# A causal attention kernel on one Trainium2 core: the diagonal key tiles of a unit are worked on first instead of last

## The chip, the cores and the metric

The kernel runs on 1 core of one Trainium2 chip. A core has five engines with their own in-order instruction queues: TensorE (PE in the profile, PEld for its weight loads), VectorE (DVE), ScalarE (ACT), GpSimd (POOL) and SyncE (SP, which here only starts DMA transfers). TensorE writes into PSUM, an accumulator memory of eight banks; VectorE and ScalarE read it from there. The metric is device time in microseconds of one execution. Before the change the median of 3 runs is 1887.55 us (1886.36 to 1890.11).

## The reference, cut to what matters

One sequence of 2048 tokens of width 256 goes through attention a, a gated feed-forward layer, attention b and the same feed-forward layer again, each on a layernormed input and each added to its input. Both attentions have 16 heads of 16 features and are causal; attention a has rotary angles, biases and 4 key heads shared by 4 query heads each, attention b has 16 key heads. The feed-forward weights arrive as 4-bit codes with scales. All is float32.

```
q, k, v = x @ Wq.T (+ bq), x @ Wk.T (+ bk), x @ Wv.T (+ bv)      # split into heads
scores = einsum('bthd,bshd->bhts', q, k) * scale
scores = where(causal, scores, -inf)
probs  = softmax(scores)                                         # exp(s - max) / sum
x = x + einsum('bhts,bshd->bthd', probs, v) @ Wo.T (+ bo)
gate, up = xn @ Wg.T, xn @ Wu.T                                  # dequantized weights
x = x + ((tanh(0.798 * (gate + 0.0447 * gate**3)) * gate * 0.5 + gate * 0.5) * up) @ Wd.T
```

## The kernel before, in words

The 2048 rows are cut into 4 query blocks of 512 rows (`b` = 0 to 3), and a block into 4 tiles of 128. Heads are worked in 4 groups of 4 (`g`). A **unit** is one (b, g); each attention has 16 units, in the order of b, then g. All instructions stand in each engine's queue in the order in which Python calls them; no scheduler moves them.

The softmax takes its maximum first, so each unit's scores are computed twice.

- **Maxima tiles** (`max_steps`, `scores`, L663 to L689). For a tile of 128 queries `i` and a key block `c`, two TensorE products (L670) make the scores of two heads, up to 512 keys wide, and one VectorE reduction (L682) takes the row maximum out of PSUM. For `c == b`, the diagonal block, the tile is only (i + 1) * 128 keys wide, and four small mask products (L645) add a large negative number to the forbidden keys. There are 8 * (b + 1) such steps. `gather` (L691) combines the maxima by five small VectorE instructions; `turn` (L708) transposes them by four TensorE products (L711) and a ScalarE copy (L717) into the tile `mT`.
- **Value steps** (`value_steps`, L724 to L815). For each tile of 128 keys `kt` and half `p` of the four heads, `pair` (L750) makes the transposed scores: two products bring in the negated maxima from `mT` (L758), two add the scores (L763), and one ScalarE exponential (L775) turns them into the tile `e`. On the diagonal key tiles (the four with kt >= 4b) only queries from `q0` on are computed (512, 384, 256 and 128 columns wide), and four mask products (L645) come between scores and exponential. `values` (L729) multiplies the exponentials of the key tile before by the values (L743) and accumulates in the one PSUM bank `ps_av`; it runs after the pair of the next key tile, one half of the queries per step, or all at once where the tile is at most 256 queries wide (`few`). A unit has 8 * (b + 1) value steps: two for each key tile.
- `end` (L786) multiplies the last key tile's exponentials and copies the sums out of `ps_av` on ScalarE (L790); `divide` (L793) transposes them (L797) and divides. Both are done in the next unit, in its steps 0 and 2.

`run` (L848) weaves these: while unit n's value steps run, the maxima tiles of unit n + 1 stand between the pair and the value products of the steps, evenly over all steps but the last three, and with them other side work: the output projection of a finished block (`out_steps`), the projections of the next block (`prep_steps`), and in attention a the dequantization of the feed-forward weights. In the last step the `turn` of unit n + 1 comes first, before that step's pair.

Three things tie the engines together around the change. Pairs and maxima tiles share three PSUM buffers `ps_s` of two banks each; a new tile waits until the ScalarE exponential or the VectorE reduction of the tile that had its buffer is done. Masked tiles are put off: their mask products and what reads them are kept in `owed` and issued by `settle` (L650) at the start of a later pair, value product or masked maxima tile. And the first pair of a unit cannot start before ScalarE has written `mT`.

Query and key rows come from DRAM: `load_q` (SP queue) for the unit after the next one, `load_k` (POOL queue) when a block's keys have been projected.

In the last query block (b = 3) `run` has no next block to prepare. The feed-forward layers (`Mlp`) follow each attention.

Of the kernel before, what the change touches and what calls it, by code (L numbers as in the profile page):

```python
# [31 lines left out]
NT = TB // P  # L32
# [47 lines left out]
def tile_hybrid_layers(  # L80
# [40 lines left out]
    def ps_s():  # L121
        return psum.tile([P, 2, 512], F32, tag="s", name="ps_s", bufs=3)
# [4 lines left out]
    def ps_m():  # L127
        return psum.tile([P, 512], F32, tag="m", name="ps_m")
# [278 lines left out]
    class Attention:  # L407
# [251 lines left out]
        def max_steps(self, b, g):  # L659

            held = {}

            def scores(i, c, p):  # L663
                if not held:
                    held["mx"] = self.wk.tile([P, NT, 4, NB], F32, tag="mx", name="mx")
                w = TB if c < b else (i + 1) * P
                self.settle("max")
                pt = ps_s()
                for r in range(2):
                    nc.tensor.matmul(  # L670
                        pt[:, r, :w],
                        lhsT=self.qT[b, g][64 * r : 64 * r + 64, p, i * P : (i + 1) * P],
                        rhs=self.key_rows(c, g, p, r, slice(0, w)),
                        start=True, stop=(c < b),
                    )

                def masked():
                    self.add_mask(pt, 0, w - P)
                    reduced()

                def reduced():
                    nc.vector.tensor_reduce(  # L682
                        held["mx"][:, i, 2 * p : 2 * p + 2, c], pt[:, :, :w], AX.X, ALU.max
                    )

                if c == b:
                    self.owed.append(("max", masked))
                else:
                    reduced()  # L689

            def gather():  # L691
                self.settle()
                nm = self.wk.tile([P, NT, 4], F32, tag="nm", name="nm")
                nc.vector.tensor_reduce(
                    nm, held["mx"][:, :, :, : b + 1], AX.X, ALU.max, negate=True
                )

                to = m_pad[:, :, :, :6].rearrange("q t r (p s) -> q t p r s", s=3)
                rest = nm.rearrange("q t (p r) -> q t p r", r=2)
                nc.vector.tensor_copy(to[:, :, :, :, 0], rest)  # L700
                less = self.wk.tile([P, NT, 2, 2], F32, tag="rest", name="rest")
                nc.vector.tensor_tensor(less, rest, to[:, :, :, :, 0], ALU.subtract)
                nc.vector.tensor_copy(to[:, :, :, :, 1], less)
                nc.vector.tensor_tensor(
                    to[:, :, :, :, 2], less, to[:, :, :, :, 1], ALU.subtract
                )

            def turn():  # L708
                pt = ps_m()
                for i in range(NT):  # L710
                    nc.tensor.matmul(  # L711
                        pt[:, i * P : (i + 1) * P],
                        lhsT=m_pad[:, i].rearrange("p r c -> p (r c)"), rhs=ident_b,
                        start=True, stop=True,
                    )
                self.mT[b, g] = self.wk.tile([P, TB], BF16, tag="mT", name="mT")
                nc.scalar.copy(self.mT[b, g], pt)  # L717


            tiles = [(i, c) for c in range(b + 1) for i in range(NT)]  # L720
            steps = [lambda i=i, c=c, p=p: scores(i, c, p) for i, c in tiles for p in range(2)]
            return steps + [gather], turn

        def value_steps(self, b, g):  # L724

            nk = NT * (b + 1)
            held = {"pending": []}

            def values(half):  # L729

                self.settle()
                kt, q0, es_ = held["pending"][0]
                few = TB - q0 <= TB // 2
                if half == 1:
                    held["pending"].pop(0)
                    if few:
                        return
                elif kt == 0:
                    held["av"] = ps_av()
                own = slice(q0, TB) if few else slice(*((q0, TB // 2), (TB // 2, TB))[half])  # L740
                for j in range(4):
                    h = g if self.first else 4 * g + j
                    nc.tensor.matmul(  # L743
                        held["av"][32 * j : 32 * j + 32, own],
                        lhsT=self.vv[kt // NT][:, kt % NT, h * VW : h * VW + 32],
                        rhs=es_[j // 2][:, j % 2, own],
                        start=(kt == 0 and half == 0), stop=(kt == nk - 1),
                    )

            def pair(kt, p):  # L750
                q0 = max(0, kt - NT * b) * P
                diagonal = kt >= NT * b
                keys = slice((kt % NT) * P, (kt % NT + 1) * P)
                self.settle()
                pt = ps_s()

                for r in range(2):
                    nc.tensor.matmul(  # L758
                        pt[:, r, q0:], lhsT=sel[64 * r : 64 * r + 64, p, :],
                        rhs=self.mT[b, g][64 * r : 64 * r + 64, q0:], start=True, stop=False,  # L760
                    )
                for r in range(2):
                    nc.tensor.matmul(  # L763
                        pt[:, r, q0:], lhsT=self.key_rows(kt // NT, g, p, r, keys),
                        rhs=self.qT[b, g][64 * r : 64 * r + 64, p, q0:],
                        start=False, stop=not diagonal,
                    )
                e = self.wk.tile([P, 2, TB], F32, tag="e", name="e", bufs=4)

                def masked():  # L770
                    self.add_mask(pt, 1, q0)
                    exponentials()

                def exponentials():
                    nc.scalar.activation(e[:, :, q0:], pt[:, :, q0:], AF.Exp, scale=QK_SCALE)  # L775

                if diagonal:
                    self.owed.append(("exp", masked))
                else:
                    exponentials()  # L780
                if p == 0:
                    held["es"] = [e]
                else:
                    held["pending"].append((kt, q0, held["es"] + [e]))

            def end():  # L786
                values(0)
                values(1)
                o = pre.tile([P, TB], F32, tag="o", name="o")
                nc.scalar.copy(o, held["av"])  # L790
                held["o"] = o

            def divide():  # L793
                o = held["o"]
                pt = ps_m()
                for i in range(NT):
                    nc.tensor.transpose(  # L797
                        pt[:, i * P : (i + 1) * P], o[:, i * P : (i + 1) * P], ident
                    )
                heads = pt.rearrange("p (t j c) -> p t j c", t=NT, c=32)  # L800
                rec = small.tile([P, NT, 4], F32, tag="rec", name="rec")
                nc.vector.reciprocal(rec, heads[:, :, :, HD])
                if g == 0:
                    self.att[b] = pre.tile([P, NT, NG, 4, HD], F32, tag="att", name="att")
                nc.vector.tensor_tensor(
                    self.att[b][:, :, g], heads[:, :, :, :HD],
                    rec.unsqueeze(3).broadcast_to([P, NT, 4, HD]), ALU.mult,
                )

            steps = []  # L810
            for kt in range(nk):
                for p in range(2):
                    scored = lambda kt=kt, p=p: pair(kt, p)
                    steps.append((scored, lambda p=p: values(p)) if kt else scored)
            return steps, end, divide  # L815

        def out_steps(self, b):
# [30 lines left out]
        def run(self, extra, beside):  # L848
# [5 lines left out]
            for n, (b, g) in enumerate(units):  # L854
# [3 lines left out]
                if g == 0 and b + 1 < NB:  # L858
                    ahead = self.prep_steps(b + 1)

                    few = -(-(len(ahead) - (7 if self.first else 5)) // 2)
# [7 lines left out]
                maxima, turn = [], None  # L869
                if n + 1 < len(units):  # L870
                    maxima, turn = self.max_steps(*units[n + 1])
                else:
                    more += beside
                steps, end, divide = self.value_steps(b, g)
# [3 lines left out]
                    steps[at] = (scored, step, *summed)  # L878
                if turn:
                    scored, summed = steps[-1]  # L880
                    steps[-1] = (turn, scored, summed)
                first = len(maxima) * 3 // len(steps)
                weave(steps[:3], maxima[:first])
                weave(steps[3:], blend(maxima[first:], more) if maxima else more, rest=3)
# [96 lines left out]
    with tc.tile_pool(name="wk1", bufs=2) as wk, tc.tile_pool(name="kv1", bufs=1) as kv:  # L981
        at.wk = at.qpool = wk
        with tc.tile_pool(name="init", bufs=1) as pool:
# [13 lines left out]
            steps, turn = at.max_steps(0, 0)  # L997
# [6 lines left out]
    with tc.tile_pool(name="kv20", bufs=1, reuse_waits="tile") as kv0, tc.tile_pool(  # L1004
# [8 lines left out]
        steps, turn = at.max_steps(0, 0)  # L1013
# [60 lines left out]
```

## Time and profile before

| | |
|---|---|
| median of 3 runs | 1887.55 us |
| the profiled execution's own time | 1890.76 us |
| its span, first to last instruction | 1888.9 us |
| mean granted TensorE clock | 0.982 |
| PE busy | 1766.7 us, 94% of the span |
| DVE busy | 1123.3 us, 59% |
| ACT busy | 805.2 us, 43% |
| attention a, from its first turn of maxima to the end of its last unit's steps | about 51 to 641 us |
| attention b, likewise | about 997 to 1548 us |

The profile is one execution; its lines name the source line, the engine, the operation, the tiles (written<-read), their shapes and how often, then busy time. "Idle before" is the time in which the engine had nothing running just before such an instruction, and the arrow names what ended it. A TensorE instruction's duration covers its whole way through the pipeline, so neighbours overlap: what an instruction costs in the queue is the distance from its start to the next one's start. Times within the execution are counted from the start of its span.

### The profile page before, as it was taken

What the parts mean: (1) busy time and instruction counts of PE and PEld (TensorE: products, weight loads), DVE (VectorE), ACT (ScalarE), POOL (GpSimd) and SP (SyncE); (2) the same over time, 40 slices, a digit from 0 to 9 for tenths busy, and PEclk for the clock granted to TensorE, in tenths of its full rate; (3) what the DMA queues carried; (4) which work ended last, traced back from release to release, by engine and by line L of the source; (5) the groups of instructions that cost most, each with busy time, mean ns of one, the idle gap of its engine ahead of it and who ended that gap; (6) DMA issues with size and microseconds to landing.
All of it is one profiled execution on the core that took longest, in us unless ns stands there. A gap on an engine that the chain in (4) does not pass through costs nothing. (4 is left out here: it accounts for less than half of the span.)

```text
span 1888.9 us, 31839 instructions
## 1 busy us (share of the span) xinstructions
PE 1766.7 (94%) x13452; PEld 928.5 (49%) x13452; DVE 1123.3 (59%) x1676; ACT 805.2 (43%) x1069; POOL 239.0 (13%) x437
## 2 busy tenths in 40 slices
PE   5788889999999999999998898999999999999999
PEld 3344444444444456656564444444444444756656
DVE  4567687778786253544445667766877715363442
ACT  1334455555667531222213355556566662131221
POOL 4111321210001011112101010010000001011110
PEclk8889999999999999999998999999999999999999
DMA  4421310310101100001303232041000010000000
GB/s 100 108 60 37 68 52 23 63 35 24 35 24 35 45 6 1 1 0 42 81 1 74 62 72 54 12 90 33 15 13 2 2 46 1 11 1 11 7 6 12
DMA packets 42271, 64.24 MB, mean 34 GB/s; under 512 B 13840, under 2 KB 20880, under 8 KB 41872
## 3 DMA queue, kind: packets, MB, share of 16 engines
q1 hardware_dynamic: 33488, 45.93, 8.2%
q0 software_dynamic: 7680, 15.74, 5.0%
q8 instruction: 106, 1.74, 0.4%
q10 hardware_dynamic: 960, 0.52, 0.1%
q14 instruction: 37, 0.30, 0.1%
HBM read 44.24 MB, written 17.83 MB: 33 GB/s over the span
## 5 line engine op out<-in xcount | busy, mean ns | idle before, releaser
L682 DVE TENSOR_REDUCE mx<-ps_s 128x2 f32<-128x1024 f32 (+3 forms) x640 | 658.2, 1060 | 221.0 <-PE ps_s L645 116.0
L775 ACT ACTIVATE e<-ps_s 128x1024 f32<-128x1024 f32 (+3 forms) x640 | 571.3, 897 | 422.6 <-PE ps_s L763 244.8
L743 PE MATMUL ps_av<-e,v 128*32 128x256 f32 (+1 forms) x4608 | 365.2, 384 | 3.4 <-ACT e L775 3.4
L763 PE MATMUL ps_s<-qT,kT 64*128 64x512 f32 (+3 forms) x1280 | 341.7, 527 | 0.0
L670 PE MATMUL ps_s<-kT,qT 64*128 64x512 f32 (+3 forms) x1280 | 269.2, 423 | 52.3 <-DVE mx L682 22.8
L758 PE MATMUL ps_s<-mT,sel 64*128 64x512 bf16 (+3 forms) x1280 | 232.7, 358 | 27.3 <-ACT mT L717 10.1
L934 PE MATMUL ps_s<-xnT,wg 128*128 128x512 f32 x512 | 242.1, 595 | 0.0
L934 PE MATMUL ps_s<-xnT,wu 128*128 128x512 f32 x512 | 240.6, 592 | 0.0
L670 PEld LDWEIGHTS ps_s<-kT,qT 64*128 64x128 f32 x1280 | 130.1, 188 | 161.6 <-ACT e L775 66.5
L758 PEld LDWEIGHTS <-sel 64*128 64x128 bf16 x1280 | 75.0, 93 | 251.2 <-issue 242.3
L942 DVE TENSOR_TENSOR t<-ps_s,t 128x512 f32<-128x512 f32 x128 | 88.1, 688 | 164.5 <-POOL t L941 162.7
L940 ACT ACTIVATE t<-ps_s 128x512 f32<-128x512 f32 x128 | 76.2, 595 | 251.8 <-PE ps_s L934 251.3
L943 ACT ACTIVATE t<-t 128x512 f32<-128x512 f32 x128 | 80.6, 629 | 200.7 <-DVE t L942 200.7
L934 PEld LDWEIGHTS ps_s<-xnT,wu 128*128 128x128 f32 x512 | 97.3, 190 | 122.7 <-issue 122.7
L941 POOL TENSOR_SCALAR t<-t 128x512 f32<-128x512 f32 x128 | 79.1, 618 | 573.0 <-ACT t L940 572.5
L743 PEld LDWEIGHTS ps_av<-e,v 128*32 128x32 f32 x4608 | 95.0, 108 | 109.1 <-issue 89.5
L934 PEld LDWEIGHTS ps_s<-xnT,wg 128*128 128x128 f32 x512 | 96.0, 192 | 106.0 <-issue 104.0
L944 DVE SCALAR_TENSOR_TENSOR t<-t,ps_s 128x512 f32<-128x512 f32 x128 | 88.0, 688 | 89.0 <-ACT t L943 89.0
L763 PEld LDWEIGHTS ps_s<-qT,kT 64*128 64x128 f32 x1280 | 130.5, 199 | 0.0
L959 PE MATMUL ps_m<-wd,inter 128*128 128x256 f32 x512 | 114.5, 380 | 0.0
L959 PE MATMUL ps_av<-wd,inter 128*128 128x256 f32 x512 | 114.5, 380 | 0.0
L959 PEld LDWEIGHTS ps_av<-wd,inter 128*128 128x128 f32 x512 | 96.7, 190 | 17.1 <-issue 4.5
(125 smaller groups left out, 1179.9 us busy)
## 6 DMA issues: line engine op xcount, KB each, us to landing
qT<-h SPq DMA_DIRECT2D x256, 64.0 KB, 2.2
kT<-h POOLq DMA_DIRECT2D x96, 128.0 KB, 5.9
h<-high SPq DMA_DIRECT2D x24, 256.0 KB, 2.6
h<-low SPq DMA_DIRECT2D x24, 256.0 KB, 2.5
wd<-wd_kept SPq DMA_DIRECT2D x2, 2048.0 KB, 7.8
wd_kept<-dq_d SPq DMA_DIRECT2D x4, 512.0 KB, 2.7
out<-x SPq DMA_DIRECT2D x16, 128.0 KB, 1.7
x<-x SPq DMA_DIRECT2D x3, 512.0 KB, 5.4
```

Of the source, the lines that this page charges most:

```text
L670: nc.tensor.matmul(pt[:, r, :w], lhsT=self.qT[b, g][64 * r : 64 * r + 64, p, i * P : (i + 1) * P], rhs=self.key_rows(c, g, p, r, slice(0, w)),
L682: nc.vector.tensor_reduce(held["mx"][:, i, 2 * p : 2 * p + 2, c], pt[:, :, :w], AX.X, ALU.max)
L743: nc.tensor.matmul(held["av"][32 * j : 32 * j + 32, own], lhsT=self.vv[kt // NT][:, kt % NT, h * VW : h * VW + 32], rhs=es_[j // 2][:, j % ...
L758: nc.tensor.matmul(pt[:, r, q0:], lhsT=sel[64 * r : 64 * r + 64, p, :], rhs=self.mT[b, g][64 * r : 64 * r + 64, q0:], start=True, stop=False,)
L763: nc.tensor.matmul(pt[:, r, q0:], lhsT=self.key_rows(kt // NT, g, p, r, keys), rhs=self.qT[b, g][64 * r : 64 * r + 64, p, q0:], start=Fals ...
L775: nc.scalar.activation(e[:, :, q0:], pt[:, :, q0:], AF.Exp, scale=QK_SCALE)
L934: nc.tensor.matmul(pt[:, k, :], lhsT=w[:, c, fc * P : (fc + 1) * P], rhs=self.xnT[b][:, c, :], start=(c == 0), stop=(c == 1),)
L941: nc.gpsimd.tensor_scalar(t, t, GELU_A, 1.0, ALU.mult, ALU.add)
L942: nc.vector.tensor_tensor(t, gate, t, ALU.mult)
L943: nc.scalar.activation(t, t, AF.Tanh, scale=GELU_C)
L944: nc.vector.scalar_tensor_tensor(t, t, 1.0, gate, ALU.add, ALU.mult)
L959: nc.tensor.matmul(po[:, :D], lhsT=inter[:, fc, i * P : (i + 1) * P], rhs=wd[:, fc, :], start=(fc == 0), stop=(fc == NFC - 1),)
```

## The change

Three orders are changed; no instruction is added, removed or resized.

1. The value steps of a unit go over the diagonal key tiles first (widest, 512 queries, to narrowest, 128), then over the full key tiles. In block 0, which has only diagonal tiles, this order stays. The flags that open and close the accumulation in `ps_av` follow the new first and last tile.
2. The maxima tiles also begin with the diagonal block, now from the widest (i = 3) to the narrowest (i = 0), then the full ones.
3. In the last step of a unit the `turn` for the next unit comes after that step's pair and before its value products, not before the pair.

```
-            tiles = [(i, c) for c in range(b + 1) for i in range(NT)]
+            tiles = [(i, b) for i in reversed(range(NT))]
+            tiles += [(i, c) for c in range(b) for i in range(NT)]
...
-            nk = NT * (b + 1)
+
+            order = [*range(NT * b, NT * (b + 1)), *range(NT * b)]
...
-                elif kt == 0:
+                elif kt == order[0]:
...
-                        start=(kt == 0 and half == 0), stop=(kt == nk - 1),
+                        start=(kt == order[0] and half == 0), stop=(kt == order[-1] and (few or half == 1)),
...
-            for kt in range(nk):
+            for kt in order:
...
-                    steps.append((scored, lambda p=p: values(p)) if kt else scored)
+                    steps.append(scored if kt == order[0] else (scored, lambda p=p: values(p)))
...
-                    steps[-1] = (turn, scored, summed)
+                    steps[-1] = (scored, turn, summed)
```

## The prediction

> **What bounds the kernel now.** First the busy times of stretches, to find the stage and its engine; only the attentions are touched. The columns are engine busy times, then the granted TensorE clock. Rows: two units of block 3 with maxima (attention b), the last unit without, and a unit (1, 3), which works on the 25 maxima steps of unit (2, 0) in 16 value steps.
>
> ```profile
> 1409.10:1455.50 46.40, 45.10 (x509) 20.38 (x506) 36.70 (x39) 30.96 (x34) 0.00 (x0) 1.00 0.05 13
> 1455.50:1502.00 46.50, 45.26 (x508) 20.16 (x504) 36.72 (x39) 30.96 (x34) 0.00 (x0) 1.00 0.01 2
> 1502.00:1548.00 46.00, 45.19 (x453) 19.03 (x450) 4.92 (x16) 33.61 (x41) 1.64 (x2) 1.00 0.13 47
> 1163.50:1193.20 29.70, 25.07 (x301) 12.61 (x298) 26.03 (x31) 14.79 (x18) 0.00 (x0) 1.00 0.07 19
> ```
>
> In block 3 PE is never idle for long; in unit (1, 3) DVE is busy for 26 of 29.7 us and bounds it. Second, who PE waits for, all over the kernel (total, times, longest):
>
> ```profile
> PE ps_s L670 <- DVE mx L682: 22.8, 47, 1.2
> PE ps_s L670 <- ACT e L775: 16.1, 31, 1.2
> ...
> PE ps_s L758 <- ACT mT L717: 10.1, 29, 0.7
> ...
> PE ps_m L711 <- DVE m_pad L704: 8.3, 7, 3.5
> ```
>
> These are small: there is little to win. Third, what a tile costs on its reader, by form:
>
> ```profile
> L682 DVE TENSOR_REDUCE mx<-ps_s 128x2 f32<-128x1024 f32 x448 | 531.3, 1220 | 122.7 <-PE ps_s L670 96.8 <-PE ps_s L645 18.9
> L775 ACT ACTIVATE e<-ps_s 128x1024 f32<-128x1024 f32 x448 | 457.1, 1026 | 311.8 <-PE ps_s L763 244.8 <-PE ps_s L645 63.4 <-PE ps_s L670 0.8
> ```
>
> Fourth, the border between two units of block 3 in order of time (start, duration, engine):
>
> ```profile
> 1409.06 0.40 PE L711 MATMUL ps_m<-ident_b,m_pad 128*128 128x128 bf16 x4
> 1409.38 0.23 PE L758 MATMUL ps_s<-mT,sel 64*128 64x128 bf16 x2
> ...
> 1409.49 0.58 ACT L717 CAST mT<-ps_m 128x512 bf16<-128x512 f32 x1 [0.45 <-PE ps_m L711]
> ...
> 1409.97 0.39 ACT L775 ACTIVATE e<-ps_s 128x256 f32<-128x256 f32 x1
> 1410.13 0.39 PE L758 MATMUL ps_s<-mT,sel 64*128 64x512 bf16 x2 [0.32 <-ACT mT L717]
> ...
> 1413.33 0.51 PE L670 MATMUL ps_s<-kT,qT 64*128 64x512 f32 x2 [0.35 <-ACT e L775]
> ...
> 1414.35 0.64 PE L743 MATMUL ps_av<-e,v 128*32 128x256 f32 x8
> ```
>
> The copy into mT runs at once, because the last pair (128 queries) and its 0.39 us exponential stand behind it; PE waits 0.32 us. From turn to the value products of step 2 it is 5.29 us here, and 5.29 to 5.30 at nearly every border behind a PE-bound unit. Fifth, two value steps with no maxima tile between, in the last unit:
>
> ```profile
> 1516.27 0.39 PE L758 MATMUL ps_s<-mT,sel 64*128 64x512 bf16 x2
> 1516.82 0.64 PE L743 MATMUL ps_av<-e,v 128*32 128x256 f32 x8
> 1516.99 1.02 ACT L775 ACTIVATE e<-ps_s 128x1024 f32<-128x1024 f32 x1 [0.20 <-PE ps_s L763]
> 1517.39 0.39 PE L758 MATMUL ps_s<-mT,sel 64*128 64x512 bf16 x2
> ```
>
> Start to start, a full pair takes PE 0.55 us before value products (0.44 before a maxima tile) and a half of value products 0.57; its exponential starts 0.72 after the pair. Such steps alternate 1.12 and 1.24 us: every second one waits 0.12 us for an exponential.
>
> **The change, part by part.** Each instruction stays, so the engines' work is the same and only waits change. I lay out the new border with the distances above.
>
> *Turn behind a full pair (A).* In blocks 1 to 3 the last pair of a unit is now full. From its start: turn at 0.55, turn lasts 0.33 (1409.06 to 1409.38), value products 0.57, so PE is ready for the next unit's first pair at 1.45. ACT has that pair's exponential first in its queue, from 0.72 to 1.74, and the mT copy behind it: starts 0.10 before its end (as 1409.97 against 1409.49 + 0.58), takes 0.58, and PE follows 0.06 later, at 2.28. PE waits 0.83 instead of 0.32: +0.51. Behind it on PE stands everything of the new unit, so nothing covers it. The last three steps, now full and without maxima, bring one 0.12 wait. +0.63 for each border behind a unit of blocks 1 to 3 with a turn, 11 an attention. The four behind the DVE-bound units (1, 3) and (2, 3) are worse: there the next reduction starts 3.29 us after the last one ends. After: the last maxima tile is issued about two reductions before its own end (-2.4), then on PE 0.33 + 0.57 + 1.12 + 1.24 + 0.55 to the turn, 1.73 to the next pair, 0.44 + 0.66 to its first reduction: 4.2; +1.0 each. 18 x 0.63 + 4 x 1.0 = **+15.3**. Bounds: 0.3 a border (+7) if exponentials run ahead, 0.9 (+20) if ACT is late. I take the middle; the rows fix it closely.
>
> *Gather waits.* Five DVE instructions before the turn now have three full steps as cover. Of the L711 waits only one stands behind a PE-bound unit of blocks 1 to 3, 0.46 us; the rest is DVE-bound (counted above), in block 0 or at the very start, where it stays: **-0.5**.
>
> *Steps 0 to 2 (B).* The pair is now masked, and the maxima tile with it is 512 wide and masked. The exponential of step 1's pair starts only when step 2 begins, and step 2's maxima tile takes its buffer: 0.80 us of waiting. Before, the ACT queue (mT, two exponentials, o, two exponentials) left 1.0 us of waiting in the same stretch: 5.29, less its work (turn 0.33, short pair with masks 0.33, three pairs 1.32, three maxima tiles 1.0, few value products 0.36, transposes 0.59: 3.93), less the wait for mT. Net **0**; bounds -0.8 and +0.4 for each of 22.
>
> *Diagonal with diagonal (C).* Before, wide maxima tiles stood beside narrow pairs; now wide with wide and narrow with narrow. Going on through steps 3 to 10 in the same way, the waits are 0.02, 0.06, 0.02, 0.16, 0.11, then 0.43 and 0.64 in steps 8 and 10: behind the 128-query tile value products are few (0.36 us, or none), while full maxima tiles come at 30 side steps in 26 steps, 1.22 us of DVE each. Sum 1.4, against 0.9 in the old diagonal stretch: +0.5. The whole unit (3, 1): pair to step 11 16.9, seventeen steps as before 24.9 and one bare 1.12, two bare 2.36, last border 2.28: 47.5 against 46.4. For 6 units of block 3 +0.5; for 12 with projections beside (PE work that fills such waits) half; for 4 DVE-bound +0.3: **+7.2**. Bounds 0 and +22.
>
> *Block 0 (8 units).* There the pair was last and narrow already: with the turn behind it the next pair still comes 1.07 us after the turn. But the maxima tiles are turned round, and steps 0 to 2 get wide beside wide: step 1's and 2's tiles wait 0.4 and 0.8 us for exponentials, while at the end narrow maxima make room earlier. I take +0.5 each, **+4**; bounds -4 and +10.
>
> *Ends and beginnings.* The two last units end on a full tile, whose value products wait for its exponential: 0.72 + 1.02 + 0.06 against 1.12 of PE work, +0.65 each, **+1.3**. The very first maxima start with the wide tile: the first reduction waits longer and DVE then runs through: **+0.4**.
>
> *DMA and other queues.* None is moved on SP or POOL. The diagonal tile needs the block's keys at the start of unit (b, 3) instead of its end: kT of block 1 landed at about 1046 us for a unit that starts at 1052, the tightest: hidden, 0; without that cover one landing of 5.9 us.
>
> Sum: 15.3 - 0.5 + 7.2 + 4 + 1.3 + 0.4 = **+27.7**. The profiled execution took 1890.76, 3.2 over the median of 1887.55; the sum made on it gives 1918.5, and on the median 1915.
>
> **The clock.** Sparse PE stretches cost clock here:
>
> ```profile
> 1070.50:1074.00 3.50, 1.85 (x26) 1.12 (x18) 1.39 (x6) 1.16 (x4) 0.00 (x0) 1.00 0.05 16
> 1074.00:1077.40 3.40, 3.40 (x22) 1.51 (x20) 2.45 (x2) 2.73 (x4) 0.00 (x0) 0.50 0.40 113
> ```
>
> With PE busy 1.85 of 3.50 us the clock is halved for the next 3.4 us: at most 1.7 us of loss. The new borders hold about 0.8 of waiting in any 3.5 us, clearly denser; I add 0 to the sum and up to 1.7 at ten sparse borders to the range. The Trainium skill ("TensorE: Matmul & The Clock Gate", section "Why this matters for your kernels") has the rule that only PE-idle gaps of more than some 3 us bring the half clock. The longest wait in that stretch is 1.33 us, so this trace disagrees. By the rule the clock term is 0 in every case; by the row it can reach 17.
>
> **Rivals.**
> 1. *Only the border pays.* The waits of C vanish because projections and ring buffers smooth them, and block 0 gains its 4: +15.3 - 0.5 + 1.7 - 4 = +12.5, **1900**. For it: PE waits of this kind are short now. Against: steps 8 and 10 have no PE work to fill.
> 2. *Heavier.* DVE comes to bound block 3's full stretch, since no narrow reductions relieve it there (C at +22), and sparse borders lose clock: 28 + 15 + 8 = +51, some +50, **1938**. For it: 1.15 x 1.22 = 1.40 us of DVE a step against about 1.4 of PE. Against: full tiles met full tiles at the same rate before.
> 3. *Faster.* The start of a unit gets the 1.14 us of value products of the full last tile as cover while ACT catches up. If step 2's tile then finds its buffer free (no 0.80) and the diagonal runs without waits (no 0.9 of before), each of 22 units gains 0.63 - 1.0 - 0.9 = -1.3: -28, **1860**. It decides where the waits from last pair to step 10 fall below the 2.3 us they are now; my layout has 3.2.
> 4. *Not what it says.* The instruction order of the built program shows the new order on PE and ACT, the mT copy behind a full exponential: excluded.
>
> **How the numbers follow.** Forecast (+14 to +44) 0.66, rival 1 and down to +4 0.13, rival 2 0.09, about nothing 0.03, faster 0.09. A difference of 0.2% (3.8 us) is about what a measurement can tell from none. Faster 0.09, same 0.04, slower 0.87. The range leaves out the upper half of rival 2, the lower half of rival 1 and the faster case: 1895 to 1938.
>
> **What would show it.** In the new profile: PE L758 waiting on mT, 10 us now, at about 0.8 a border, some 20; L775 of 128x1024 directly ahead of L717 on ACT; L670 waiting on ACT e up, its longest about 0.8 in step 2; unit (3, 1) from turn to turn 47.5 us; busy time of every engine as now. I am wrong if the unit is under 46.4 us, which would mean that steps 0 to 10 wait less than I laid out, or if the granted clock falls under 0.97.

## The result, and the profile after

| | before | after |
|---|---|---|
| median of 5 runs | 1887.97 us (1886.36 to 1890.11) | 1937.57 us (1933.25 to 1939.7) |
| the profiled execution's own time | 1890.76 us | 1933.25 us |
| its span | 1888.9 us | 1931.5 us |
| granted clock of that execution | 0.982 | 0.981 |

The change makes the kernel slower by 49.6 us: a ratio of 1.026, 95% interval 1.0249 to 1.0272. The forecast was 1915, so its direction holds and its size does not: the time lies just inside the upper end of the range, at the figure of rival 2. Profile against profile the loss is 42.5 us. The profiled execution of after is the quickest of its five, and has the highest clock of them (0.981; the others 0.977 to 0.973). Of the 7.1 us between the two figures, 4.3 come from this (its time lies that far under the median of after), and 2.8 from the profiled execution of before, which lies that far over its median.

First the work. Line 1 of the page of after, with busy time, share of the span and number of instructions of each engine:

```profile
PE 1774.8 (92%) x13452; PEld 923.6 (48%) x13452; DVE 1118.3 (58%) x1676; ACT 810.5 (42%) x1069; POOL 238.5 (12%) x437
```

Within 9 us this is what each engine did before: the time is lost in waiting. The stretches that the prediction listed, from turn to turn in after (two units of block 3 with maxima, the last unit, unit (1, 3); busy times of PE, PEld, DVE, ACT and POOL, then the clock):

```profile
1448.70:1496.30 47.60, 45.34 (x506) 19.95 (x504) 36.51 (x39) 31.25 (x34) 0.00 (x0) 1.00 0.05 13
1496.30:1543.80 47.50, 45.11 (x507) 20.06 (x505) 36.52 (x39) 31.26 (x34) 0.00 (x0) 1.00 0.01 2
1543.80:1589.80 46.00, 44.89 (x457) 18.70 (x456) 4.23 (x15) 34.36 (x41) 1.65 (x2) 1.00 0.13 47
1189.60:1222.20 32.60, 27.36 (x298) 13.28 (x296) 26.12 (x31) 14.88 (x18) 0.00 (x0) 0.95 0.06 18
```

The block 3 units went from 46.4 and 46.5 to 47.6 and 47.5 us, as laid out, with the same DVE time. Unit (1, 3) went from 29.7 to 32.6 us, also with the same DVE time (26.0 and 26.1): the engine that bounds it now stands still for 6.5 us instead of 3.7. Whom PE waits for in after (total, times, longest; L670, L711 and L717 keep their numbers, the pair's L758 is now L760, L763 is L765, L743 is L745, L775 is L777, L790 is L792, L797 is L799):

```profile
PE ps_s L670 <- DVE mx L682: 36.3, 79, 1.2
PE ps_s L670 <- ACT e L777: 28.5, 45, 1.0
PE ps_s L760 <- ACT mT L717: 21.9, 32, 0.8
...
PE ps_s L760 <- ACT e L777: 10.4, 27, 0.8
...
PE ps_m L711 <- DVE m_pad L704: 2.0, 1, 2.0
```

The wait for `mT` went from 10.1 to 21.9 us (some 20 was the sign to look for), as predicted. The gather wait fell from 8.3 to 2.0, further than the 0.5 us in the sum. The waits of maxima tiles grew by 13.5 us (for reductions) and 12.4 us (for exponentials), which is more than the prediction had room for.

The border ahead of a block 3 unit in after, in order of time (start, duration, engine; idle before and its releaser in brackets):

```profile
1448.17 0.39 PE L760 MATMUL ps_s<-mT,sel 64*128 64x512 bf16 x2
...
1448.72 0.40 PE L711 MATMUL ps_m<-ident_b,m_pad 128*128 128x128 bf16 x4
...
1448.89 1.02 ACT L777 ACTIVATE e<-ps_s 128x1024 f32<-128x1024 f32 x1 [0.22 <-PE ps_s L765]
...
1449.05 0.64 PE L745 MATMUL ps_av<-e,v 128*32 128x256 f32 x8
...
1449.82 0.58 ACT L717 CAST mT<-ps_m 128x512 bf16<-128x512 f32 x1
1450.45 0.39 PE L760 MATMUL ps_s<-mT,sel 64*128 64x512 bf16 x2 [0.75 <-ACT mT L717]
...
1454.96 0.45 PE L670 MATMUL ps_s<-kT,qT 64*128 64x384 f32 x2 [0.78 <-ACT e L777]
```

The last full pair starts at 1448.17, its exponential 0.72 later, the copy into `mT` 1.65 later, the next unit's pair 2.28 later. In between PE has only the value products of 1449.05 to issue and waits 0.75. The last row is the maxima tile of step 2, with the predicted wait (0.80 laid out, 0.78 here).

Where the time went, as differences of turn-to-turn times (profile after minus profile before), beside what the prediction's terms give for the same units:

| units | predicted | measured |
|---|---|---|
| 6 of block 3 with maxima | 6 x (0.63 + 0.5) = 6.8 | 6.7 |
| 4 bound by VectorE: (1, 3), (2, 3) in both attentions | 4 x (1.0 + 0.3) = 5.2 | 12.5 |
| 12 of blocks 1 and 2 with projections beside them | 12 x (0.63 + 0.25) = 10.6 | 15.3 |
| 8 of block 0 | 4 | 9.4 |
| the rest (feed-forward, ends) | 1.2 | -1.3 |
| span | 27.8 | 42.6 |

In the terms a border belongs to the unit ahead of it; in time most of it lies behind the turn, in the next unit. Moved there, the forecast is 4 x (0.63 + 0.3) = 3.7 for the four VectorE-bound units, 10.0 for the twelve and 7.5 for the six of block 3: the gaps at the first two only widen.

### The profile page after: what moved, and what is told of

It reads as the page before. It is cut to its first block, busy times and chain, and to the rows that moved or that the text cites. A ratio compares the mean times of both kernels' runs of the same rounds, so it can differ in the third digit from the quotient of the medians.

```text
span 1931.5 us, 31836 instructions
## 1 busy us (share of the span) xinstructions
PE 1774.8 (92%) x13452; PEld 923.6 (48%) x13452; DVE 1118.3 (58%) x1676; ACT 810.5 (42%) x1069; POOL 238.5 (12%) x437
## 5 line engine op out<-in xcount | busy, mean ns | idle before, releaser
L777 ACT ACTIVATE e<-ps_s 128x1024 f32<-128x1024 f32 (+3 forms) x640 | 572.4, 896 | 473.0 <-PE ps_s L645 254.7
L745 PE MATMUL ps_av<-e,v 128*32 128x256 f32 (+1 forms) x4608 | 363.6, 384 | 4.3 <-ACT e L777 4.3
L670 PE MATMUL ps_s<-kT,qT 64*128 64x512 f32 (+3 forms) x1280 | 280.2, 432 | 77.4 <-DVE mx L682 36.3
L765 PE MATMUL ps_s<-qT,kT 64*128 64x512 f32 (+3 forms) x1280 | 340.7, 526 | 0.0
L760 PE MATMUL ps_s<-mT,sel 64*128 64x512 bf16 (+3 forms) x1280 | 232.0, 357 | 44.2 <-ACT mT L717 21.9
L670 PEld LDWEIGHTS ps_s<-kT,qT 64*128 64x128 f32 x1280 | 128.8, 188 | 190.3 <-DVE mx L682 78.4
L760 PEld LDWEIGHTS <-sel 64*128 64x128 bf16 x1280 | 73.7, 93 | 268.8 <-issue 266.3
L745 PEld LDWEIGHTS ps_av<-e,v 128*32 128x32 f32 x4608 | 99.4, 109 | 126.2 <-issue 99.1
L765 PEld LDWEIGHTS ps_s<-qT,kT 64*128 64x128 f32 x1280 | 130.2, 198 | 0.0
```

What stands on the lines that cost most here:

```text
L670: nc.tensor.matmul(pt[:, r, :w], lhsT=self.qT[b, g][64 * r : 64 * r + 64, p, i * P : (i + 1) * P], rhs=self.key_rows(c, g, p, r, slice(0, w)),
L745: nc.tensor.matmul(held["av"][32 * j : 32 * j + 32, own], lhsT=self.vv[kt // NT][:, kt % NT, h * VW : h * VW + 32], rhs=es_[j // 2][:, j % ...
L760: nc.tensor.matmul(pt[:, r, q0:], lhsT=sel[64 * r : 64 * r + 64, p, :], rhs=self.mT[b, g][64 * r : 64 * r + 64, q0:], start=True, stop=False,)
L765: nc.tensor.matmul(pt[:, r, q0:], lhsT=self.key_rows(kt // NT, g, p, r, keys), rhs=self.qT[b, g][64 * r : 64 * r + 64, p, q0:], start=Fals ...
```

## The experiments

The change has three parts: the value order (V), the maxima order (M) and the turn behind the pair (T). The first theory was that most of the loss is the border of A, a full exponential ahead of the `mT` copy. Its rivals were that the value order or the maxima order costs inside the units, wherever the turn stands.

### One part undone

**Turn first** (V and M stay):

```
-                    steps[-1] = (scored, turn, summed)
+                    steps[-1] = (turn, scored, summed)
```

> The change with its third edit undone: the turn comes before the last pair again; both orders stay new. Theory A (the border: the copy into mT stands behind a full exponential): the waits of L758/L760 on mT, 21.9 us in all, fall under 4 us, since pair (0.55) and value products (0.57) cover the 0.58 us copy, and the time falls by 22 borders x 0.83 = 18 us, to about 1919 (1913 to 1924). Theory B (the maxima order, diagonal beside diagonal, costs the time, and ScalarE and VectorE make PE wait a little later anyway): over 1930.

Measured 1914.49 us (1910.05 to 1916.6) against 1887.62 before on the same chip: ratio 1.0134 (1.0112 to 1.0157). The waits for `mT` fall from 21.9 us to 3.0 (7 times), and PE-bound units of block 3 fall back to within 0.4 us of before. In the new order the turn's place is worth 23 us. But 27 us of loss stay, with no border to blame.

**Old maxima order** (V and T stay):

```
-            tiles = [(i, b) for i in reversed(range(NT))]
-            tiles += [(i, c) for c in range(b) for i in range(NT)]
+            tiles = [(i, c) for c in range(b + 1) for i in range(NT)]
```

> The change with its second edit undone: maxima tiles in the old order (full ones first, diagonal last, narrow to wide); value order and turn are new. Theory A: the border waits stay (mT about 22 us); only the eight units of block 0 (+9.4 us in the profiles) and the 1.1 us inside each of four VectorE-bound units come back: 1920 to 1928. Theory B: most of the loss goes, 1895 to 1905.

Measured 1932.07 us (1927.38 to 1937.73), ratio 1.0235 (1.0206 to 1.0264). Only 5.5 us come back; the `mT` waits stay at 21.9 us. With V in, full maxima tiles stand beside narrow pairs, and block 3 units get longer still: attention b's (3, 0) to (3, 2) are 1.68, 1.55 and 1.47 us over before from turn to turn, against 1.09, 1.18 and 0.93 in after. Undoing M here removes one cost and adds another.

**Old value order** (M and T stay):

```
-            order = [*range(NT * b, NT * (b + 1)), *range(NT * b)]
+            nk = NT * (b + 1)
...
-            for kt in order:
+            for kt in range(nk):
```

> The change with its first edit undone: value steps in the old order (diagonal last); maxima order and turn are new. Theory A: the last pair is narrow again and its masked exponential is issued after the copy into mT, so the border is as before; what stays is block 0 and full maxima beside narrow pairs at a unit's end: 1890 to 1902. Theory B: the loss stays, 1920 to 1938.

Measured 1917.21 us (1915.12 to 1918.18), ratio 1.0153 (1.0138 to 1.0168). A clear miss: with narrow last pairs, nothing like 30 us should have been left. The theory that the border carries the loss falls in this simple form. The parts cost something each by itself.

### One part alone

So each part was put alone into the kernel before: the value order with its accumulation flags; the maxima order; and the turn behind the pair.

> Only the first edit: value steps with the diagonal first; maxima and turn as before. Theory A (the edits' costs add up; the turn behind a full pair was 20 to 23 us of it): the time of the run with old maxima order, 1932, less 22 borders x 0.9 = 1912 (1906 to 1917). Theory C (new value order costs nothing once the turn is first, the rest is the maxima order): 1887 to 1895.

> Only the second edit: maxima tiles with the diagonal first, widest first; value steps and turn as before. Theory A: the run with old value order (1917) less what the late turn costs with a narrow last pair, 22 x 0.33 = 7: about 1910; the full maxima tiles then end beside the narrow pairs of a unit's end, where VectorE (1.22 us each) has no PE work beside it. Theory C: as e1, 1914, since the value order would cost nothing. A maxima order that costs nothing would give 1888.

> Only the third edit: the turn after the last pair; both orders as before. Theory A: the last pair (0.33 us with its masks) no longer runs beside the copy into mT, so the next unit's first pair comes 0.33 us later wherever the maxima were gathered in time: 20 x 0.33 = +6.6, 1894 (1890 to 1897). If the turn's place alone were the cost: over 1905.

| edits | median, us | over before | ratio (95%) |
|---|---|---|---|
| V | 1911.37 (1910.37 to 1912.26) | +23.5 | 1.0127 (1.0113 to 1.0141) |
| M | 1909.36 (1906.25 to 1912.76) | +21.5 | 1.0111 (1.0096 to 1.0126) |
| T | 1896.74 (1892.34 to 1898.13) | +8.9 | 1.0046 (1.0031 to 1.006) |
| V, M | 1914.49 | +26.9 | 1.0134 |
| V, T | 1932.07 | +44.5 | 1.0235 |
| M, T | 1917.21 | +29.6 | 1.0153 |
| V, M, T | 1937.57 | +49.6 | 1.026 |

All three alone came out where they were expected. Two readings follow from the table by subtraction. T costs 8 to 9 us where the last pair is narrow (T alone 8.9; after M 8.1) and 21 to 23 us where it is full (after V 21.0; after V and M 22.7, or 23.1 without the difference of the two medians of before): that fits the mechanism of A, a full exponential ahead of the copy. And M costs 21.5 us on the old value order but 3.4 on the new one: V and M do not add up. The six units of block 3 with maxima show it at full clock: V alone makes them 4.1 us longer in all, M alone 2.0, both together 1.0. That diagonal beside diagonal fits better than either order against its opposite is the likely reason; no run shows it by itself.

### The copy on another engine

If ScalarE's queue is what makes the border, the copy into `mT` on VectorE should end it, with all three edits in:

```
-                nc.scalar.copy(self.mT[b, g], pt)
+                nc.vector.tensor_copy(self.mT[b, g], pt)
```

> The whole change, but the copy into mT is made by VectorE instead of ScalarE. Theory A (ScalarE's in-order queue makes the wait): VectorE is idle for some 3 us before the turn in most units, so the copy runs right behind the turn and the mT waits (21.9 us) fall under 4 us; 1937.6 - 18 = about 1919 (1913 to 1925). Theory B: over 1930.

Measured 1929.95 us (1929.45 to 1933.82), ratio 1.0227 (1.021 to 1.0244): 7.6 us better than after, less than half of what was expected (its median clock, 0.972, is the lowest of all the kernels here). The same border in this kernel:

```profile
1445.52 0.40 PE L711 MATMUL ps_m<-ident_b,m_pad 128*128 128x128 bf16 x4
...
1445.69 1.02 ACT L776 ACTIVATE e<-ps_s 128x1024 f32<-128x1024 f32 x1 [0.21 <-PE ps_s L764]
1445.85 0.64 PE L744 MATMUL ps_av<-e,v 128*32 128x256 f32 x8
1445.95 0.69 DVE L717 CAST mT<-ps_m 128x512 bf16<-128x512 f32 x1 [2.48 <-PE ps_m L711]
1446.70 0.39 PE L759 MATMUL ps_s<-mT,sel 64*128 64x512 bf16 x2 [0.21 <-DVE mT L717]
```

The copy now starts as soon as the turn is done, beside the exponential: from turn to next pair 1.18 us instead of 1.72 in after. So at this border ScalarE's queue made 0.54 of the 0.75 us. The other 0.21 stays: the turn behind the pair leaves only the value products (0.57 us in the queue) to cover the transposes' way out and a copy that takes 0.69 us on VectorE, 0.58 on ScalarE. The expectation had counted the wait as gone; all waits for `mT` fell from 21.9 to 11.1 us, half.

### Where the orders cost

Next, all three edits everywhere but in the units of the last head group (g = 3) of blocks 0 to 2, which keep the old orders and the old turn; four of these six are the VectorE-bound units of the prediction. A unit's `new` also sets the order of the maxima that are worked on beside it:

```
+                new = g < 3 or b == 3
...
+            if not new:
+                tiles = [(i, c) for c in range(b + 1) for i in range(NT)]
...
+            order = [*range(NT * b, NT * (b + 1)), *range(NT * b)] if new else [*range(NT * (b + 1))]
...
+                    steps[-1] = (scored, turn, summed) if new else (turn, scored, summed)
```

> The whole change, except in the units with g = 3 of blocks 0 to 2 (they work on the maxima of the next block, 8 tiles more than they have value steps, and VectorE bounds them); these six units keep all three old orders. Theory A (what was under-sized lies in these units: +3.53, +3.07, +2.95, +2.97 in the two later blocks and +1.52, +2.30 in block 0, by the profiles): 1937.6 - 16.3 = about 1921 (1916 to 1926). Theory E (the excess over the forecast is clock and noise, spread over all units): over 1928.

Then block 0 and the very first maxima keep the old ones as well:

```
-                new = g < 3 or b == 3
+                new = b > 0 and (g < 3 or b == 3)
```

> As the run before, and the other units of block 0 and the very first maxima keep the old orders too; new orders remain in blocks 1 to 3 with g < 3 and in the last unit. Theory A: another 5.5 us less (the six units' growth in the profiles): about 1915 (1910 to 1920); what remains is 12 units with projections beside (+15.3 in the profiles), 6 of block 3 (+6.7) and ends. Theory E: over 1924.

And last, the same with the turn first everywhere, so that the new orders stand alone in the PE-bound units of blocks 1 to 3:

```
-                    steps[-1] = (scored, turn, summed) if new else (turn, scored, summed)
+                    steps[-1] = (turn, scored, summed)
```

> As the run before (new orders only in blocks 1 to 3 with g < 3 and in the last unit), and there too the turn is first in the last step. Theory A: 18 borders lose the 0.83 us wait behind a full exponential, 15 us: 1911.6 - 15 = about 1897 (1893 to 1901); what is left over the kernel before, some 9 us, is the two orders themselves, beside projections above all. If the turn were cheap in these units (the wait made good a step later): over 1905.

Measured 1917.14 us (1913.64 to 1919.08), ratio 1.0156 (1.014 to 1.0171); 1911.64 (1909.17 to 1913.75), ratio 1.0128 (1.0115 to 1.0142); and 1891.92 (1890.15 to 1896.77) against 1889.09 before, ratio 1.003 (1.0017 to 1.0043). The first two lie in their ranges; the last lies below its range. Some 9 us were expected to be left for the two orders: where VectorE does not bound the unit, in blocks 1 to 3, they cost about 3. The border in that last kernel shows what the turn's place does there, with a full last pair in both:

```profile
1416.24 0.40 PE L711 MATMUL ps_m<-ident_b,m_pad 128*128 128x128 bf16 x4
1416.57 0.39 PE L762 MATMUL ps_s<-mT,sel 64*128 64x512 bf16 x2
...
1416.68 0.58 ACT L717 CAST mT<-ps_m 128x512 bf16<-128x512 f32 x1
1417.12 0.64 PE L747 MATMUL ps_av<-e,v 128*32 128x256 f32 x8
...
1417.69 0.39 PE L762 MATMUL ps_s<-mT,sel 64*128 64x512 bf16 x2
```

The copy runs while PE does the pair and the value products, and the next unit's pair comes 1.45 us after the turn, without a wait: exactly the 1.45 at which the prediction had PE ready. After needs 2.28 us for the same work, 0.83 more; over 18 borders 15 us, which is the difference of the two profiles (spans 1910.0 and 1894.9). By medians it is 19.7, but the median clocks differ too (0.9815 and 0.985).

An account of the 49.6 us, by differences of medians:

- the two orders in the eight units of block 0 (where only the maxima order changes) and the four VectorE-bound ones: 1914.49 - 1891.92 = 22.6; the median clocks differ here as well (0.9765 and 0.985)
- the turn behind the pair at the 18 other borders behind units of blocks 1 to 3: 1911.64 - 1891.92 = 19.7
- the turn behind the pair at the borders behind those twelve units: (1937.57 - 1911.64) - 22.6 = 3.3
- the two orders in the other units of blocks 1 to 3: 1891.92 - 1889.09 = 2.8

These four are bound to add up to 1937.57 - 1889.09, so their sum of 48.4 is no proof; the rest of the 49.6 is the difference between two medians of before. The runs behind each median spread by 4 to 7 us.

What happens in a VectorE-bound unit shows on VectorE's own rows. First unit (1, 3) of attention b in before, from the gather ahead of it to its first reductions:

```profile
1162.28 0.23 DVE L704 TENSOR_TENSOR m_pad<-rest,m_pad 128x16 bf16<-128x16 f32 x1
1165.51 4.62 DVE L682 TENSOR_REDUCE mx<-ps_s 128x2 f32<-128x1024 f32 x4 [2.99 <-PE ps_s L670]
1170.04 0.25 DVE L802 RECIPROCAL rec<-ps_m 128x16 f32<-128x16 f32 x1
```

The same in after:

```profile
1185.79 0.23 DVE L704 TENSOR_TENSOR m_pad<-rest,m_pad 128x16 bf16<-128x16 f32 x1
1192.82 3.22 DVE L682 TENSOR_REDUCE mx<-ps_s 128x2 f32<-128x1024 f32 x3 [6.79 <-PE ps_s L645]
1197.22 0.26 DVE L804 RECIPROCAL rec<-ps_m 128x16 f32<-128x16 f32 x1 [1.18 <-PE ps_m L799]
```

The turns ahead are at 1163.47 and 1189.58, so the first reduction comes 3.24 instead of 2.04 us behind the turn: the `mT` wait, and masks ahead of it, since the first maxima tile is a diagonal one. After the first three reductions VectorE runs dry once more for 1.18 us, where before it ran through: the masked maxima tile of step 2 waits 0.41 us for a put-off exponential, and its masks stand behind the transposes of `divide`. From the first reduction's start to the last one's end it is 27.46 instead of 26.39 us, and from there to the next turn 1.94 instead of 1.3. That makes 1.2 + 1.07 + 0.65 = 2.9 us, all of what this unit lost. The other three VectorE-bound units lose in the same three places: all four 1.20 to 1.25 us at the start, 0.30 to 1.78 inside and 0.50 to 1.46 at the end, 12.5 us in all.

A lower clock is not needed for it. Unit (2, 3) of attention b from turn to turn, before and after (columns as above), has the full clock and the same VectorE time in both, and still loses 3.0 us:

```profile
1317.72:1357.51 39.79, 36.34 (x412) 17.06 (x409) 35.48 (x39) 22.97 (x26) 0.00 (x0) 1.00 0.05 14
1353.33:1396.09 42.76, 38.35 (x410) 17.33 (x409) 35.47 (x39) 23.07 (x26) 0.00 (x0) 1.00 0.05 13
```

### The turn earlier instead

T puts the turn later. The opposite, in the kernel before alone, is the turn one step earlier, behind the pair of the last step but one:

```
-                    scored, summed = steps[-1]
-                    steps[-1] = (turn, scored, summed)
+                    scored, summed = steps[-2]
+                    steps[-2] = (scored, turn, summed)
```

> The kernel before with the turn one step earlier: after the pair of the last step but one and before its value products; both orders as before. Theory A (PE waits 0.32 us a border for the copy into mT because only 0.33 us of PE work stands behind the turn): value products (0.57) and the last pair (0.33) now cover the copy, the waits of L758 on mT fall from 10 us to under 4, and about 18 borders x 0.32 = 6 us go: 1882 (1879 to 1886). Theory D (the gather is not ready a step earlier): L711 waits for m_pad rise by as much, 1886 to 1892.

Measured 1886.97 us (1882.52 to 1893.89, 11 runs), ratio 0.9996 (0.9985 to 1.0007): no difference. The `mT` waits nearly vanish (1.3 us), PE-bound units are 0.4 us shorter each, but the turn now meets maxima that aren't gathered yet, above all where VectorE is late. The wait for the gather in this kernel (8.3 us, 7 times, in before):

```profile
PE ps_m L711 <- DVE m_pad L704: 17.4, 14, 3.5
```

So the step earlier was kept only where the gather is ready, in blocks 1 to 3 without g = 3:

```
+                    if b > 0 and g < 3:
+                        scored, summed = steps[-2]
+                        steps[-2] = (scored, turn, summed)
+                    else:
+                        scored, summed = steps[-1]
+                        steps[-1] = (turn, scored, summed)
```

> The kernel before with the turn one step earlier only in units of blocks 1 to 3 with g < 3, where the gather is ready by then; elsewhere as before. Theory A: the units that lost 0.4 us each in the run with the turn earlier everywhere do so again (about 14 of them) and the ones that gained waits for the gather do not: 1887.8 - 5.8 = 1882 (1879 to 1885). If run-to-run clock is all there is to see: 1887 to 1889.

Measured 1882.26 us (1879.22 to 1887.23, 12 runs) against 1887.51: ratio 0.9973 (0.9964 to 0.9981), as expected and quicker than both kernels. Waits in this kernel:

```profile
PE ps_m L711 <- DVE m_pad L704: 11.3, 11, 3.5
...
PE ps_s L758 <- ACT mT L717: 4.7, 13, 0.7
```

The `mT` waits are halved, the gather waits cost 3 us more, and 13 of the units are 0.37 to 0.47 us shorter (from one division to the next).

## Why the prediction was right or wrong

**The border (A): right in mechanism, and in size at the border that was laid out.** The layout had PE wait for `mT` 0.83 us and the next pair 2.28 us behind the last; the profile has 0.75 and 2.28. The two kernels that differ only in the turn's place there (1911.64 and 1891.92) confirm it as a cause. At the four borders behind VectorE-bound units it was not right in size (below). What the layout left out is that the value order with the turn first would have been better than before at this place: the new border against the old is +0.63, but against a turn ahead of the full pair it is +0.83. That is why T costs more behind V than the 15 us of A.

**Gather waits: too small a term, at no cost. Steps 0 to 2 (B): right.** 2.0 us of gather waits are left, those at the very start. The waits in block 0 (3.2 us before) are gone too, which the sum did not count; block 0 grew all the same. The wait in step 2 is 0.78 against 0.80.

**Diagonal with diagonal (C) in block 3: right as a net, and partly by luck.** Six units took 6.7 us more against 6.8, unit (3, 1) from turn to turn 47.6 against 47.5. But with the turn first, V and M leave these six only 1.0 us over before, 0.16 each, with a border that by the line above is 0.20 better than the old one (0.83 - 0.63). So C costs some 0.36 us a unit and not 0.5. The turn behind the pair adds 0.95, which makes the new border some 0.75 over the old one and not 0.63. Two small errors cancel.

**The VectorE-bound units: the step that failed.** The terms were +1.0 at the border behind such a unit and +0.3 inside, 5.2 us for four. They measured 12.5. The prediction had said itself that DVE bounds unit (1, 3), and then priced everything ahead of and inside it by PE's waits, scaled down. There a wait of PE counts through when the next reduction can start: in unit (1, 3) of attention b +1.2 at the unit's own beginning (priced as +0.63), +1.07 inside, where 0.3 was taken, +0.65 at its end ahead of the turn. The +1.0 at the border behind such a unit can be held against the trace: from the last reduction to the next unit's first it was to go from 3.29 to 4.2 us and went to 4.57, 5.26, 4.76 and 5.54, a mean of +1.7. In medians, the two orders in these units and in block 0 cost 22.6 us; an estimate by the clock's price below puts some 7 of these down to the lower clock of the first of the two kernels.

**Block 0: right in sign, mis-sized.** +0.5 a unit was taken, between -0.5 and +1.25; 9.4 us for eight is +1.17 each, near the upper bound. It was taken near the middle, although no row showed maxima turned round. M alone makes these eight 8.2 us longer in its profile, so the turned maxima carry most of it.

**Projection units: mis-sized.** 15.3 against 10.6. In the last kernel of "Where the orders cost" (turn first, VectorE-bound units and block 0 old) the twelve are 3.5 us over before, 0.3 each; with the border that is 0.20 better there, this puts C at some 0.5 and not at the 0.25 taken. So the half taken off for projections that fill the waits does not seem to be there, though single units lie between -3.5 and +3.2 us, and no run shows it by itself. With the turn still first and both orders new everywhere the twelve are 8.1 us over before, and the turn behind the pair brings them to 15.3. The step from 3.5 to 8.1 comes with the new orders of the units around them, and no term was laid out for it. The clock differs between these profiles (0.982, 0.976, 0.981), and how much of the steps is clock stays open.

**Ends: small.** From the last turn to the end it is 0.7 us more, against 0.65; the first turn is 0.1 later, against 0.4. From the last turn of attention a to the first of attention b it is 2.2 us less, which no term had and no run explains.

**DMA: right.** The earlier use of the new block's keys brought no wait; the one for queries is 10.4 us in after and 10.3 before.

**The clock: left at 0 in the sum, kept in the range.** Over the five runs of after the time rises by 0.8 us for each 0.001 of granted clock lost (1933.25 at 0.981, 1939.7 at 0.973). Their median clock is 0.975, against 0.983 for the kernel before; 0.008 makes some 6 us. It is an estimate, since a lower clock and a longer wait can also have one cause. The borders did stay at full clock, as argued; the windows that lost it were elsewhere (below).

**Rival 2 had the time, not the reason.** Its 1938 is the result within 1 us. But its main part, VectorE bounding the full stretch of block 3, did not happen: those units lost what the forecast said. Heavier it was, in the units that VectorE bounded already. Rival 1 is excluded by the time and by block 0, which lost 9.4 us where it was to win 4. Rival 3 is excluded by the 0.78 us in step 2. The profile's clock, 0.981, did not fall under the 0.97 named as a sign of error either; the medians show the smaller fall that the profile, as the quickest run, does not.

What stays open: why M costs 21.5 us beside the old values. Its loss is spread over block 0, the g = 3 units and the units with projections, mostly 0.2 to 2.4 us a unit, and no run separates masks that come earlier from reductions that come wide first. And the share of clock and waiting in the medians was not told apart by a run. For the VectorE-bound units the traces bound it: in after only the two units (1, 3) have half clock, 3.4 us each, at most 1.7 us of loss apiece, and M alone makes the four units 7.0 us longer without any.

## What to carry to other kernels

Price a change of order in each stage on the engine that bounds it: where VectorE is the bound, lay out when its next reduction can start, and read its own idle time, not PE's waits; a delay at the start of such a stage has nothing to hide it. A small copy that the next stage waits for must not stand behind a long activation in the same queue, and the best place for what feeds it is as early as its input is surely ready: one step earlier in 18 of the units won 5 us, one step earlier everywhere won nothing. The costs of two orders need not add up: here 23.5 and 21.5 us apart, 26.9 together.

## What the runs showed of the hardware

The clock can fall without any long pause of TensorE. Three stretches of after, in unit (1, 3) of attention b (length, then busy times of PE, PEld, DVE, ACT, POOL, then the granted clock):

```profile
1203.00:1206.40 3.40, 2.95 (x38) 1.42 (x40) 3.40 (x4) 0.98 (x2) 0.00 (x0) 1.00 0.00 0
1206.40:1209.90 3.50, 2.15 (x20) 1.09 (x18) 3.50 (x4) 1.04 (x2) 0.00 (x0) 1.00 0.00 0
1209.90:1213.30 3.40, 3.15 (x22) 1.61 (x20) 3.00 (x3) 1.39 (x2) 0.00 (x0) 0.51 0.00 0
```

PE's rows in the second of them, where DVE is busy throughout:

```profile
1206.43 0.46 PE L670 MATMUL ps_s<-kT,qT 64*128 64x512 f32 x2
1207.41 0.50 PE L670 MATMUL ps_s<-kT,qT 64*128 64x512 f32 x2 [0.52 <-DVE mx L682]
...
1208.52 0.39 PE L760 MATMUL ps_s<-mT,sel 64*128 64x512 bf16 x2 [0.54 <-ACT e L777]
...
1209.67 0.58 PE L670 MATMUL ps_s<-kT,qT 64*128 64x512 f32 x2 [0.29 <-DVE mx L682]
```

The longest wait is 0.54 us, PE is busy for 61% of the 3.5 us, and then the clock is halved for the next 3.4 us. Other stretches ahead of a halved one in after have PE busy for 1.77 to 2.06 of 3.5 us (271.20 to 274.70 us: 2.06, longest wait 0.95). At the border shown above PE is busy for 2.75 of 3.5 us (1448.20 to 1451.70), in spite of its longer single wait of 0.75, and keeps the full clock. A low busy share does not always bring it: in before, PE is busy for 1.93 of 3.4 us (377.70 to 381.10, 57%, longest wait 1.17), and the clock of the next 3.4 us is full. So these rows give no sharp limit.

With the new value order the VectorE-bound units (1, 3) pay in clock too. Their half-clock time (twice the missing clock times the length, from turn to turn) is 3.4 to 17.1 us in the profiles of the five kernels that have the new value order there, and none in before and the eight others; units (2, 3) have none in any. The median clock goes the same way: 0.972 to 0.9765 with the new value order there, 0.981 to 0.985 without.

The Trainium skill ("TensorE: Matmul & The Clock Gate", section "A second HAM failure mode: psum-queue depth-cycling") says that frequent short pauses between groups of matmuls can make the clock go back and forth, and these rows agree. The rule that the prediction took from the same page, no idle gaps of more than some 3 us, is not enough to keep the clock, as they show; that only such gaps bring the half clock, as the prediction put it, they contradict.
